# First product of a graph layer: pauses of the second and third part's ordering without work of the part behind them, and own-edge products one block behind VectorE

## The chip, the cores and the metric

The kernel runs on one core of a Trainium2 chip. The metric is the device time of one execution in microseconds (us). One execution was taken by the hardware profiler; every stretch and duration below is from it, with times counted from the start of its span. Engines are named as in the profile: PE (TensorE, matrix products), PEld (its weight loads), DVE (VectorE), ACT (ScalarE), POOL (GpSimd), SP (SyncE, which only issues transfers here).

## The reference, cut to what matters

```python
def _spmm_plus_eye(rows, cols, vals, X):          # 12500 rows of 256, 212500 edges
    msgs = vals[:, None] * X[cols]
    return jax.ops.segment_sum(msgs, rows, num_segments=N) + X
support = feature @ W1
out = _spmm_plus_eye(rows, cols, vals, support)
out = _batchnorm_relu(out, gamma, beta)
out = _spmm_plus_eye(rows, cols, vals, out @ W2)
x = x + gnn(layernorm(x), src, dst, edge_weight)
x = x + moe(layernorm(x))                          # 8 experts, the best 2 of each row
```

The edges come in no useful order for the chip: the kernel orders them itself by target row. 12500 of them are own edges (source row = target row); the rest are drawn at random.

## The kernel before

**The ordering.** The edges lie in 13 slots of 128 x 128, cut into four parts of 2, 3, 4 and 4 slots (`parts[0]` to `parts[3]`, called a, b, c, d here). Each part is ordered on the chip by a network of compare-and-exchange steps (`network`, L783). One `exchange` is, on DVE, a comparison (L641), a minimum (L643), a maximum (L645) and two predicated copies (L648, L650); ACT copies one operand of each pair aside first (L628, L632, L633). Between some steps the layout is turned by `swap` (L724): PE transposes into PSUM (L731) and ACT copies back (L734, L737). Before that come the keys (`make_keys`, L573, seven DVE instructions over the whole part). After it, ACT's counts (L598) are summed (`counted`, L601), the starts of the tiles are worked out (`begins`, L887) and the ordered list goes to DRAM slot by slot (`decode`, L848, stores at L867).

**The first product** (`spmm4`, L365) takes the lists one after the other: a, b, c, then d. It works in blocks of 128 edges: 269, 391, 513 and 513 of them. One block is a gather of 128 table rows on POOL (L215, `gt`), a selection matrix made by DVE six blocks ahead (L420, `sel`) and one to a few products on PE (L463). Every 11 to 21 blocks (four target tiles) SP loads a stretch of the list (L383), PE transposes it (L393) and DVE writes the gather's row numbers (L404, `wat`) and two more rows (L406, L408); DVE adds finished tiles (L1220). `gt` has 12 buffers, `sel` 10.

**What stands beside it.** While list a is multiplied, part b is ordered; beside b, part c; beside c, part d. The order of the instructions is written out by hand: after each block `beside()` (L1271) calls `now.give(RATE[i])`, with `RATE` 1.3, 1.15 and 1.05 us per block in the three stages. A `Beside` (L1032) keeps a ledger: what it was allowed and what it has spent, in estimated us that the generators yield (an exchange of n columns counts 0.1 + 0.00104 n for each of its first three instructions). It issues work until spent reaches allowed. A generator yields `SWAP` = 5.0 and `LEAD` = 2.5 where it has to wait for a turning; until the allowance has caught up, it issues nothing. `settle()` finishes an exchange that stands half done, and `rest()` (L1068), called after the last block of a stage, issues all that is left before the next stage begins.

**Fills.** A `Beside` with a `fill` hands the allowance on while it pauses:

```python
            if not self.gens or self.spent > self.allowed + LEAD / 2:
                if self.fill:
                    self.fill.give(us)
                return
```

L1176 makes c the fill of b and d the fill of c; L1240 makes the merging of a and b the fill of d. So c may be worked on while b pauses, and d while c pauses or is done. In the third stage (i = 2) d's generators are followed by the offsets of all lists (`beyond_all`, L1229) and by the own-edge weights of lists a, b and c (L1269).

**Own edges.** `self_weights` (L1015) loads the end of a list, where the own edges stand, and adds their weights into `selfw`, 128 rows by 98 tiles. For each block of 128 edges (18, 25, 33 and 33 for the four lists) `self_block` (L248) makes two matrices on DVE, `sel` (L251) and `tosel` (L253), and PE multiplies them into one PSUM tile (L254); both matrices come from a pool of two buffers. One addition (L1029) ends each list. List d's own edges are done beside the fourth product (L1377), at 1.0 us per block, with the rest issued when the second group of tiles begins.

Behind the third stage stand two loops over what did not fit (`self_beyond`, L266, and `beyond`, L219). They ran no turn in this execution, but all engines read their counts and branch there. The fourth product, the first projection and the merging of the lists follow, then batch norm, the second product and the experts.

Of the kernel before, what the change touches and what calls it, by code (L numbers as in the profile page):

```python
# [9 lines left out]
F32 = mybir.dt.float32  # L10
# [14 lines left out]
def kernel(  # L25
# [30 lines left out]
    nc = tc.nc  # L56
# [188 lines left out]
                    to = acc_flat[:, ds(col, F)]  # L245
                    nc.vector.tensor_tensor(to, pg, to, op=ALU.add)

    def self_block(pool, row, tile, w, ps, first, last):  # L248

        sel = pool.tile([P, P], F32, name="sel")  # L250
        nc.vector.tensor_single_scalar(sel, iota_row, row, op=ALU.is_equal)  # L251
        to = pool.tile([P, NT], F32, name="tosel")
        nc.vector.tensor_scalar(to, iota_t, tile, w, op0=ALU.is_equal, op1=ALU.mult)  # L253
        nc.tensor.matmul(ps, sel, to, start=first, stop=last)  # L254

    def self_rows(pool, win, n):

        at = pool.tile([P, 2, n], I32, name=f"sat{n}")
        rt = pool.tile([P, 2, n], F32, name=f"srt{n}")
        nc.vector.tensor_copy(at[:, 0, :], win[:, :, 1].bitcast(F32))  # L260
        nc.vector.tensor_single_scalar(at[:, 1, :], at[:, 0, :], LG, op=ALU.logical_shift_right)
        nc.vector.tensor_single_scalar(at[:, 0, :], at[:, 0, :], P - 1, op=ALU.bitwise_and)
        nc.vector.tensor_copy(rt, at)
        return rt

    def self_beyond():  # L266


        with tc.tile_pool(name="slp", bufs=1) as op, \
                tc.tile_pool(name="ps_v", bufs=1, space=PSUM) as pso:  # L270
            n = nc.values_load(most[0:1, 1:2], min_val=0, max_val=E // P + 1)
            with tc.For_i(0, n, 1):
                for lst in lists:
                    at = nc.values_load(lst.selfs[0:1, 1:2], engines=(mybir.EngineType.SP,),
                                        min_val=0, max_val=lst.FRONT + lst.size)
                    win = op.tile([P, 1, 3], I32, name="win")
                    nc.sync.dma_start(win[:, 0, :], lst.edges[ds(at, P), :])
                    rt = self_rows(op, win, 1)
                    ps = pso.tile([P, NT], F32, name="ps")
                    self_block(op, rt[:, 0, :], rt[:, 1, :], win[:, 0, 2:3].bitcast(F32), ps, True,  # L280
                               True)
                    nc.vector.tensor_tensor(selfw, selfw, ps, op=ALU.add)
                    nc.vector.tensor_scalar(lst.selfs[:, 1:2], lst.selfs[:, 1:2], P,
                                            lst.FRONT + lst.size, op0=ALU.add, op1=ALU.min)
# [496 lines left out]
    SWAP, LEAD = 5.0, 2.5  # L781

    def network(p, ring):  # L783

        for k in range(1, LG):
            for j in reversed(range(k)):
                yield from exchange(p, bit(j, k))
                yield "step"
        for j in reversed(range(LG)):
            yield from exchange(p, bit(j))  # L790
            yield "step"
        where, top = p.where, (p.n - 1).bit_length()
        for k in range(LG + 1, 2 * LG + top + 1):
            r = k - 2 * LG
            yield LEAD
            if r < 0:
                swap(p, ring, row_bits(k - LG - 1))
            elif r == 0:
                swap(p, ring, row_to_slot)
            else:  # L800
                swap(p, ring, slot_signs({where[i] for i in range(1 << top) if where[i] is not None
                                          and ((i >> (r - 1)) ^ (i >> r if r < top else 0)) & 1}))
            yield SWAP
            for j in reversed(range(r)):
                prs = slot_step(where, j, lambda i: r < top and i >> r & 1)
                yield from exchange_slots([((p, a), (p, b)) for a, b in prs])
                yield "step"
            for j in reversed(range(min(LG, k - LG))):
                yield from exchange(p, bit(j))
                yield "step"  # L810
            yield LEAD
            swap(p, ring)
            yield SWAP
            for j in reversed(range(LG)):
                yield from exchange(p, bit(j))
                yield "step"
# [198 lines left out]
    def self_weights(lst, pool, pairs, psl):  # L1015

        at = nc.values_load(lst.starts[0:1, lst.NS:], engines=(mybir.EngineType.SP,), min_val=0,
                            max_val=lst.FRONT + lst.size)
        win = pool.tile([P, lst.NSB, 3], I32, name=f"swin{lst.name}")
        nc.sync.dma_start(win, lst.edges[ds(at, lst.NSB * P), :].rearrange("(p b) r -> p b r", p=P))  # L1020
        yield SWAP
        ps = psl.tile([P, NT], F32, name="psl")
        rt = self_rows(pool, win, lst.NSB)
        yield 0.8
        for b in range(lst.NSB):
            self_block(pairs, rt[:, 0, b:b + 1], rt[:, 1, b:b + 1], win[:, b, 2:3].bitcast(F32), ps,
                       b == 0, b == lst.NSB - 1)
            yield 0.7
        nc.vector.tensor_tensor(selfw, selfw, ps, op=ALU.add)  # L1029
        yield 0.3  # L1030

# [60 lines left out]
    with ExitStack() as stack, tc.tile_pool(name="ln", bufs=1) as lp, tc.manual_schedule():  # L1092
# [80 lines left out]
        nc.vector.memset(less, 0.0)  # L1173

        work = [Beside(p.make_keys(), network(p, ringb)) for p in parts]
        work[1].fill, work[2].fill = work[2], work[3]  # L1176
        for c in parts[0].make_keys():
            pass
        clock, first, half = 0.0, 12.0, None
# [61 lines left out]
        for i in range(3):  # L1241
# [26 lines left out]
            if i == 2:  # L1268
                now.gens += [beyond_all()] + [self_weights(lst, slp, sap, psl) for lst in lists[:3]]  # L1269
# [12 lines left out]


    self_beyond()
    beyond(lists, most[0:1, 0:1], tab1)
    stats = accp.tile([P, KF, len(groups), nc.vector.BN_STATS_DIM], F32, name="stats")
    with ExitStack() as stack, tc.manual_schedule():
# [85 lines left out]

        back = Beside(merges())
        selfb = Beside(self_weights(lists[3], slp, sap, psl))

        def beside():  # L1377
# [36 lines left out]
    with tc.tile_pool(name="bn1", bufs=1) as b1p, \  # L1414
# [11 lines left out]
        for g0, n in groups:  # L1426
# [3 lines left out]
            for c0 in range(0, n, 2):  # L1430
                m = min(2, n - c0)
                ps = psb.tile([P, 2, F], F32, name="ps")
                for c in range(c0, c0 + m):
                    for k in range(KF):
                        nc.tensor.matmul(ps[:, c - c0, :], accT[:, k, g0 + c, :], wg2[:, k, :],
                                         start=(k == 0), stop=(k == KF - 1))
# [234 lines left out]
```

## Time and profile before

| | |
|---|---|
| median of 11 runs | 4880.34 us (4869.77 to 4885.23) |
| profiled execution | 4875.12 us, span 4873.4 us |
| mean granted PE clock over the span | 0.947 |
| busy over the span | PE 83%, PEld 58%, DVE 72%, ACT 31%, POOL 68% |
| gathers of the first product | 1686, mean 978 ns |
| own-edge products (L254) | 109 blocks |

How to read it: shares are over the whole span, whose second half (experts) has other limits than the stages of the first product. A time of "idle before" belongs to the engine that waited, with what ended the wait behind the arrow. A wait for several things is put down to the last of them.

### The profile page before, as it was taken

The page shows a single profiled execution, that of the slowest core. Times are in us where ns is not written, and L with a number is a line of the kernel's source. Part 1 is how long each engine was busy: PE and PEld are TensorE (multiplying, and loading weights), DVE is VectorE, ACT ScalarE, POOL GpSimd, SP SyncE. Part 2 cuts the span into 40 slices and gives each one's busy share as a digit, 9 for nine tenths or more (in the row PEclk, how much of TensorE's full clock was granted, in tenths as well). Part 3 has the DMA queues.
Part 4 walks back from the last instruction along what each step waited for, and adds up shares of the span by engine and source line. Part 5 has one row for each costly group of instructions (what it writes and reads, how often), then busy time and mean ns, then how long its engine had stood idle before and what let it go on. Part 6 is the DMA issues. An engine that isn't in the chain of part 4 may idle for free. (4 is left out here: it accounts for less than half of the span.)

```text
span 4873.4 us, 60974 instructions
## 1 busy us (share of the span) xinstructions
PE 4059.7 (83%) x15678; PEld 2843.8 (58%) x15678; DVE 3487.6 (72%) x11649; ACT 1532.5 (31%) x3783; POOL 3332.2 (68%) x3364
## 2 busy tenths in 40 slices
PE   0167768887777778888787899999999999999999
PEld 0045545554444455555465667767777777777777
DVE  9888988888787857676744566666666666666666
ACT  4767655654555001111130111211211212212223
POOL 0067757777777767777735777777777777777772
PEclk9998888989898889999998999999999999999999
DMA  4333333333333433343454343343343433433431
GB/s 134 110 90 99 98 87 106 106 111 104 106 106 105 110 100 118 118 121 117 117 175 135 113 126 115 112 126 115 113 128 114 126 116 114 127 115 115 125 106 48
DMA packets 284573, 551.61 MB, mean 113 GB/s; under 512 B 78202, under 2 KB 176612, under 8 KB 284100
## 3 DMA queue, kind: packets, MB, share of 16 engines
q0 software_dynamic: 160656, 438.91, 31.0%
q1 hardware_dynamic: 119684, 103.53, 7.0%
q10 hardware_dynamic: 3888, 5.24, 0.3%
q8 instruction: 134, 2.20, 0.2%
q14 instruction: 211, 1.73, 0.1%
HBM read 503.54 MB, written 43.91 MB: 112 GB/s over the span
## 5 line engine op out<-in xcount | busy, mean ns | idle before, releaser
L215 POOL DMA_INDIRECT gt<-tab,wat x1686 | 1648.9, 978 | 837.7 <-DMA raw<-lista 262.9
L215 POOL DMA_INDIRECT gt<-tab,win x1661 | 1680.7, 1012 | 626.7 <-issue 236.1
L463 PE MATMUL pg<-gt,sel 128*128 128x256 f32 x4826 | 1474.5, 434 | 346.9 <-DMA gt<-tab,wat 234.1
L463 PEld LDWEIGHTS pg<-gt,sel 128*128 128x128 f32 x4826 | 912.9, 210 | 791.6 <-DVE sel L420 187.8
L343 PE MATMUL pg<-gt,sel 128*128 128x256 f32 x3322 | 893.8, 387 | 92.7 <-DMA gt<-tab,win 50.5
L343 PEld LDWEIGHTS pg<-gt,sel 128*128 128x128 f32 x3322 | 620.5, 192 | 372.3 <-issue 121.4
L1581 PE MATMUL ph<-tT,w1s 128*128 128x512 f32 (+3 forms) x1728 | 742.8, 554 | 2.0 <-ACT h L1583 2.0
L1590 PE MATMUL py<-w2s,h 128*128 128x256 f32 x3136 | 744.4, 381 | 0.0
L1595 DVE SCALAR_TENSOR_TENSOR y<-py,cmb,y 128x256 f32<-128x256 f32 x784 | 343.9, 479 | 558.1 <-PE py L1590 557.6
L1583 ACT ACTIVATE h<-ph,b1s 128x512 f32<-128x512 f32 (+3 forms) x432 | 278.8, 647 | 1273.5 <-PE ph L1581 1270.0
L420 DVE TENSOR_SCALAR sel<-iota_all,wrel,wwt 128x128 f32<-128x128 f32 (+1 forms) x1686 | 630.1, 388 | 53.4 <-PE pg L463 52.3
L1590 PEld LDWEIGHTS py<-w2s,h 128*128 128x128 f32 x3136 | 600.2, 192 | 81.4
L210 DVE TENSOR_SCALAR sel<-iota_all,rel,win 128x128 f32<-128x128 f32 x1661 | 532.5, 370 | 127.4 <-PE pg L343 117.6
L1581 PEld LDWEIGHTS ph<-tT,w1s 128*128 128x128 f32 x1728 | 322.8, 191 | 203.2 <-issue 169.2
L1573 DVE SCALAR_TENSOR_TENSOR y<-b2s,cmb,y 128x256 f32<-128x256 f32 x784 | 328.3, 480 | 0.2
L731 PE MATMUL pt<-ident,keya 128*128 128x128 f32 x40 | 12.6, 416 | 218.1 <-DVE keya L645 211.1
L731 PEld LDWEIGHTS pt<-ident,keya 128*128 128x128 f32 x40 | 6.6, 207 | 223.8 <-issue 189.8
L1220 DVE TENSOR_TENSOR acc<-pg,acc 128x512 f32<-128x512 f32 x147 | 101.1, 688 | 33.4 <-PE pg L463 33.2
L1344 DVE BATCH_NORM_STATS2 stats<-po 128x6 f32<-128x512 f32 (+1 forms) x50 | 34.2, 684 | 125.8 <-ACT acc L1339 125.7
L1583 ACT ACT_TABLE_LOAD x53 | 68.0, 1283 | 174.7 <-PE ph L1581 174.6
L641 DVE TENSOR_TENSOR maskd<-keyd,opk 128x256 uint16<-128x256 f32 (+1 forms) x154 | 59.1, 383 | 56.9 <-ACT opk L628 51.0
L1336 PE MATMUL po<-aT,wg 128*128 128x512 f32 (+1 forms) x200 | 94.4, 594 | 4.7 <-DVE stats L1344 2.3
(448 smaller groups left out, 4310.3 us busy)
## 6 DMA issues: line engine op xcount, KB each, us to landing
gt<-tab,wat POOLq DMA_INDIRECT x1686, 2.8
gt<-tab,win POOLq DMA_INDIRECT x1661, 2.8
tab<-acc SPq DMA_DIRECT2D x48, 512.0 KB
own<-tab SPq DMA_DIRECT2D x46, 512.0 KB
acc<-in_x_dram SPq DMA_DIRECT2D x24, 512.0 KB
y<-in_x_dram SPq DMA_DIRECT2D x22, 512.0 KB
out_dram<-y SPq DMA_DIRECT2D x22, 512.0 KB
listm<-rec ACTq DMA_DIRECT2D x13, 192.0 KB
```

Source lines behind the costliest of these rows:

```text
L210: nc.vector.tensor_scalar(sel, iota_row, rel, w, op0=ALU.is_equal, op1=ALU.mult)
L215: nc.gpsimd.indirect_dma_start(out=gt, out_offset=None, in_=table, in_offset=bass.IndirectOffsetOnAxis(ap=at, axis=0))
L343: nc.tensor.matmul(state["ps"], sels.pop(0), gt, start=(j == 0), stop=(j == lst.blocks(t) - 1))
L420: nc.vector.tensor_scalar(sel[:, :n * P], iota_all[:, (mine[0] - g0) * P:(mine[-1] - g0 + 1) * P], rel[:, b:b + 1], w[:, b:b + 1], op0=ALU ...
L463: nc.tensor.matmul(ps[:, t - pair, :], sel[:, i * P:(i + 1) * P], gt, start=False, stop=not left)
L1220: nc.vector.tensor_tensor(acc[:, t:t + m, :], ps[:, :m, :], acc[:, t:t + m, :], op=ALU.add)
L1336: nc.tensor.matmul(po[:, :T], wg1[:, k, j * P:(j + 1) * P], aT[0][:, k, :T], start=(k == 0), stop=(k == KF - 1))
L1573: nc.vector.scalar_tensor_tensor(y[:, c, :], b2s[:, e, :], v["cmb"][:, c, e:e + 1], y[:, c, :], op0=ALU.mult, op1=ALU.add)
L1581: nc.tensor.matmul(ph[:, :T], w1s[:, e, k, j * P:(j + 1) * P], v["zT"][:, k, :T], start=(k == 0), stop=(k == KF - 1))
L1583: nc.scalar.activation(v[e][:, j, :T], ph[:, :T], AF.Gelu, bias=b1s[:, e, j:j + 1])
L1590: nc.tensor.matmul(py[:, c - c0, :], v[e][:, k, c * P:(c + 1) * P], w2s[:, e, k, :], start=(k == 0), stop=(k == KF - 1))
L1595: nc.vector.scalar_tensor_tensor(y[:, c, :], py[:, c - c0, :], v["cmb"][:, c, e:e + 1], y[:, c, :], op0=ALU.mult, op1=ALU.add)
```

## The change

L1176 goes, so that neither c nor d is any other part's fill; the merging stays the fill of d. `self_block` only makes its two matrices and hands them back. In `self_weights` the product of block b - 1 is issued after the matrices of block b, one more turn of the loop issues the last product, each turn is charged 1.0 in place of 0.7, and a `SWAP` of 5.0 is charged ahead of the addition. `self_beyond` keeps its order.

```diff
-    def self_block(pool, row, tile, w, ps, first, last):
+    def self_block(pool, row, tile, w):
...
         nc.vector.tensor_scalar(to, iota_t, tile, w, op0=ALU.is_equal, op1=ALU.mult)
-        nc.tensor.matmul(ps, sel, to, start=first, stop=last)
+        return sel, to
...
-        for b in range(lst.NSB):
-            self_block(pairs, rt[:, 0, b:b + 1], rt[:, 1, b:b + 1], win[:, b, 2:3].bitcast(F32), ps,
-                       b == 0, b == lst.NSB - 1)
-            yield 0.7
+        made = []
+        for b in range(lst.NSB + 1):
+            if b < lst.NSB:
+                made.append(self_block(pairs, rt[:, 0, b:b + 1], rt[:, 1, b:b + 1],
+                                       win[:, b, 2:3].bitcast(F32)))
+            if b:
+                nc.tensor.matmul(ps, *made.pop(0), start=(b == 1), stop=(b == lst.NSB))
+            yield 1.0
+        yield SWAP
         nc.vector.tensor_tensor(selfw, selfw, ps, op=ALU.add)
...
         work = [Beside(p.make_keys(), network(p, ringb)) for p in parts]
-        work[1].fill, work[2].fill = work[2], work[3]
```

Both programs hold the same instructions; only their order on each engine differs.

More of the change, by code (lines that the diff above doesn't have):

```diff
@@ L279, in self_beyond @@
                     ps = pso.tile([P, NT], F32, name="ps")
-                    self_block(op, rt[:, 0, :], rt[:, 1, :], win[:, 0, 2:3].bitcast(F32), ps, True,
-                               True)
+                    sel, to = self_block(op, rt[:, 0, :], rt[:, 1, :], win[:, 0, 2:3].bitcast(F32))
+                    nc.tensor.matmul(ps, sel, to, start=True, stop=True)
                     nc.vector.tensor_tensor(selfw, selfw, ps, op=ALU.add)
```

## The prediction

> **What bounds the kernel now.** The change touches the first product, so I read that stage by stage, not the shares of the span. First view: the busy time of each engine in the four products and the three gaps between them (start:end, length, then PE, PEld, DVE, ACT, POOL, PE clock).
>
> ```profile
> 265.90:623.70 357.80, 276.90 (x1039) 193.49 (x1039) 326.25 (x1195) 255.63 (x860) 258.12 (x269) 0.88 0.35 100
> 623.70:650.10 26.40, 8.61 (x24) 5.59 (x23) 18.21 (x77) 10.76 (x34) 0.02 (x1) 0.56 0.10 32
> 650.10:1142.30 492.20, 396.45 (x1458) 258.41 (x1458) 428.20 (x1439) 277.87 (x798) 373.33 (x391) 0.90 0.37 108
> 1142.30:1145.90 3.60, 2.12 (x9) 1.03 (x8) 1.04 (x5) 0.42 (x2) 0.03 (x1) 0.93 0.14 39
> 1145.90:1797.60 651.70, 513.51 (x1822) 321.88 (x1822) 506.44 (x1820) 231.50 (x641) 493.60 (x513) 0.89 0.37 106
> 1797.60:1809.90 12.30, 2.45 (x9) 1.04 (x8) 2.61 (x10) 0.00 (x0) 0.05 (x2) 0.63 0.11 29
> ```
>
> No engine is full in the second and third product, and yet they can't go faster: the timeline of POOL shows gathers of 0.95 us with 0.30 us between them, start to start 1.25 (median 1.251), and never less.
>
> ```profile
> 1794.17 0.95 POOL L215 DMA_INDIRECT gt<-tab,wat  x1 [0.30 <-issue]
> 1795.42 0.95 POOL L215 DMA_INDIRECT gt<-tab,wat  x1 [0.30 <-PE pg L463]
> 1796.67 0.95 POOL L215 DMA_INDIRECT gt<-tab,wat  x1 [0.30 <-PE pg L463]
> 1809.87 1.05 POOL L215 DMA_INDIRECT gt<-tab,wat  x1 [12.25 <-DVE sel L420]
> ```
>
> So the gathers alone need 269 x 1.251 = 336.5, 391 x 1.251 = 489.1, 513 x 1.251 = 641.8 us. Against that the products took 357.8 (21 more), 492.2 (3 more) and 651.7 (10 more). Only in the first does something else set the pace. The waits of that window say what:
>
> ```profile
> POOL gt L215 <- DVE wat L404: 14.6, 7, 4.1
> POOL gt L215 <- DVE wwt L408: 6.2, 2, 3.9
> DVE maskc L641 <- ACT opk L628: 18.7, 14, 2.7
> ```
>
> POOL waited 20.8 us in 9 places for the row numbers, behind which DVE was late, and DVE itself stood 18.7 us in c's exchanges for ACT's copies. One such place in the timeline of all engines:
>
> ```profile
> 481.40 0.29 DVE L650 COPY_PREDICATED wtsc<-maskc,opw 128x128 f32<-128x128 uint16 x1
> 481.60 0.17 DVE L404 TENSOR_SCALAR wat<-pt 128x11 int32<-128x11 int32 x1
> ...
> 482.04 0.95 POOL L215 DMA_INDIRECT gt<-tab,wat  x1 [3.95 <-DVE wwt L408]
> ```
>
> Work of part c, put into a pause of b, stands directly ahead of the row numbers. The gaps between products count in full: POOL is idle, and all that follows waits.
>
> **The change part by part.** The ledger first, as it decides where each instruction stands; it follows from the costs in the code. Before, c and d entered the second and third product, their own, with 45.4 and 100.2 us already spent; now with nothing.
> - The second product allows 391 x 1.15 = 449.7; c's keys, network, counts and list sum to 443.7. It fits: c's list ends at block 386 of 391 (before at 349).
> - The third allows 513 x 1.05 = 538.7. Before, 590.0 - 100.2 = 489.8 fell due in it, done at block 468. Now d's 100.2 come back, the own edges of a, b, c are charged 76 x 0.3 + 3 x (1.0 + 5.0) = 40.8 more, and 16.8 fall away, since 21 more counts go with the blocks and not as 0.8 each: 614. About 75 don't fit: 23 of b's 25 own-edge blocks and all 33 of c's (29.3 and 45.1 with what stands around them), 56 blocks. `rest()` issues them after the last gather.
>
> *First product, -18.3.* 154 DVE instructions of c and d go: 14 exchange steps of ten (2.0 us each, as from 625.4 to 627.4) and two sets of keys (3.8 us each, the first from 312.7), 36 us together, and with them the 18.7 us of waits. DVE falls from 326 to some 290 of 336. I leave 3 of the 21 us, what the second product loses at about the same DVE share: 339.5 instead of 357.8. Bounds: -21 and, if b's own dense stretches fill DVE, 0.
>
> *Gap 623.7 to 650.1, -4.* One exchange of c stands in it (625.4 to 627.4, 2 us) and DVE enters it late: the turning of b that belongs to block 263 ran at 622.6, as the last gather did. Bounds -7 and 0.
>
> *Second product, 0* (-3 to +3): gathers bound it, DVE loses work.
>
> *Gap 1142.3 to 1145.9, +1.* The chain from b's count (the memset L604 at 639.59) to the next gather (650.08) takes 10.5 us; c's fourth slot adds a store, some 2 us. It now starts at block 381, ten gathers (12.5 us) before the end, plus 2.9 us from a gather's start to its product. It comes out level with the 3.6 us that the last products cost anyway. Bounds 0 and +10.5.
>
> *Third product, -1.5.* DVE gets some 24 us more (272 instructions of d, 65 us, against the pairs of 62 own-edge blocks, 30, and merging, 11): about 530 of 642. Its dense stretches stay as they were. The 10 us of loss lie mostly around 1600 to 1700, offsets and a's own edges, where POOL waited 2.4 us once for the products L254; those are now charged 1.0. Bounds -10 and +5.
>
> *Gap 1797.6 to 1809.9, +43.* Now DVE is idle here: its last addition starts at 1800.29, list d is loaded at 1805.70, row numbers at 1807.95. With the change DVE's queue holds 56 blocks of own edges between that addition and the loops, and every engine branches in those loops before d's first load. No gather hides it. The nearest row is the run of such blocks at 1838.8 to 1845.8, where only they are issued. First DVE's timeline, starts of `sel`:
>
> ```profile
> 1842.20 0.29 DVE L251 TENSOR_SCALAR sel<-iota_all,srt 128x128 f32<-128x128 f32 x1
> ...
> 1843.07 0.43 DVE L251 TENSOR_SCALAR sel<-iota_all,srt 128x128 f32<-128x128 f32 x1 [0.32 <-PE psl L254]
> ...
> 1843.59 0.29 DVE L251 TENSOR_SCALAR sel<-iota_all,srt 128x128 f32<-128x128 f32 x1
> ...
> 1844.44 0.32 DVE L251 TENSOR_SCALAR sel<-iota_all,srt 128x128 f32<-128x128 f32 x1 [0.32 <-PE psl L254]
> ```
>
> Then the window, with PE and PEld first and the granted clock, 0.50, third from the end:
>
> ```profile
> 1842.20:1845.80 3.60, 3.31 (x11) 2.60 (x11) 2.13 (x9) 0.00 (x0) 2.69 (x4) 0.50 0.34 97
> ```
>
> Its fastest blocks take 0.44, DVE's own pace; the last three average 0.75, at clock 0.50, where DVE waits for the product that frees the two buffers. PE's last eight products took 5.34 us, 0.67 each; I take that: 56 x 0.67 = 37.5. The new order changes nothing here, as nothing stands between the products on PE. Added: c's row numbers 0.9, two additions that wait for the last product 2 x 1.1. Sum 40.6. Behind the loops four exchanges of the merging (a and b, twice) remain, 5.1 us by b's 1.54 and a's 1.0, against 2.25 us that DVE waits there now: +2.9. Together 43; bounds 56 x 0.44 and 56 x 0.75, so +30 to +48. Below that a gain is excluded: the queue is in order.
>
> [...] The row shows the array at half clock within such a run, though PE was busy for 3.31 of 3.60 us. [...]
>
> *Fourth product, +1* (-3 to +5). By block 21 six fewer of d's 33 own-edge blocks are made, so the burst at 1838.8 grows from 11 to 17 blocks, 4 us; gathers run up to 12 blocks ahead and did not wait there before. PE's waits for `tosel` shrink (11.0 us in 7 places, no gather behind most).
>
> Sum: -18.3 - 4 + 0 + 1 - 1.5 + 43 + 1 = **+21 us**. On the profiled execution's 4875.1 (span 4873.4) that is 4896; it ran 5.2 us under the median of 4880.3, so I forecast 4901 for the median.
>
> **The rivals.**
> - *VectorE's pace sets the tail.* 56 x 0.44 = 24.6 instead of 37.5: +8, 4888, no change. For: DVE was the slower engine at clock 0.93. Against: the clock fell within 4 us.
> - *The first stage keeps its waits* (b alone saturates DVE, which was 95% busy from 266 to 320, nearly without c): no -18 and no -4, +43, 4923. Against: each wait followed work of c or d.
> - *List c comes late*, if its count slips behind the last gather: 10 us more, 4911, and 4924 if the whole 26.4 us gap of list b repeats.
> - *Faster: VectorE gets to the tail before the gathers end.* It is idle for 145 of 652 us in the third product; if it ran over 31 us ahead (past -0.2%), and with all 43 hidden, the sum is -22, 4858. Against: block 2 of the tail needs the buffer that the product of block 0 frees, which PE reaches behind the last gather's landing.
>
> **How the numbers follow.** Chances: forecast 0.62, VectorE's pace 0.13, waits kept 0.12, list c late 0.08, tail hidden 0.05. A measurement of this kernel tells about 0.2% (10 us) from no change: faster 0.05, same 0.15 (the second case and the low edge of the first), slower 0.80. The range runs from +2, under the case at VectorE's pace, to +42, just below waits kept: 4882 to 4922. The forecast's own range is 4890 to 4911.
>
> **What would show it.** First product near 340, no POOL wait on L404 there; second 492; gap behind it under 6; third near 650; the gap before list d near 55, with 56 own-edge blocks in it. I am wrong if the clock stays open in that gap (then 40 to 46), or if the gap isn't there at all.

## The result and the profile after

The changed kernel takes 4896.71 us (median of 8 runs, 4892.48 to 4903.23) against 4880.30 before (31 runs): a ratio of 1.0037, 95% interval 1.0029 to 1.0046. It is slower by 16.4 us; 4901 was forecast. The profiled execution has a span of 4890.6 us, 17.2 more than before (4873.4).

The same view as before the change: busy time by stretch (start:end, length, then PE, PEld, DVE, ACT, POOL, granted PE clock). The first six lines answer to the six of the kernel before, the seventh is the fourth product.

```profile
265.70:603.70 338.00, 283.01 (x1052) 186.99 (x1052) 294.65 (x1050) 236.39 (x782) 256.34 (x269) 0.90 0.37 106
603.70:624.90 21.20, 3.67 (x14) 1.90 (x12) 13.08 (x57) 6.66 (x20) 0.00 (x0) 0.64 0.12 38
624.90:1118.00 493.10, 403.24 (x1430) 259.63 (x1430) 406.28 (x1331) 251.79 (x718) 374.28 (x391) 0.87 0.37 107
1118.00:1122.00 4.00, 2.91 (x12) 1.41 (x10) 1.04 (x5) 0.00 (x0) 0.04 (x2) 0.96 0.24 66
1122.00:1769.50 647.50, 514.49 (x1732) 317.01 (x1732) 533.60 (x1954) 276.61 (x805) 491.50 (x513) 0.86 0.38 107
1769.50:1827.00 57.50, 37.60 (x125) 28.79 (x124) 36.21 (x148) 2.83 (x9) 0.00 (x0) 0.51 0.06 16
1827.00:2508.80 681.80, 568.87 (x2057) 366.02 (x2058) 478.34 (x1537) 104.35 (x239) 523.57 (x513) 0.92 0.41 121
```

The view shows a gain and a loss of nearly twice its size. The first product fell from 357.8 to 338.0 and the gap behind it from 26.4 to 21.2: 25 us gained. The gap before list d grew from 12.2 to 57.5: 45.3 lost. The other stretches moved by 4.3 us at most.

The gain: these are POOL's waits in the first product (us in total, times, longest). The 20.8 us behind the row numbers (L404, L408) are gone; what is left is 0.30 between two gathers.

```profile
POOL gt L215 <- issue: 41.1, 135, 0.3
POOL gt L215 <- PE pg L463: 32.3, 106, 0.3
```

The loss: POOL's timeline around the gap, the last gather of the third product and the first of the fourth.

```profile
1768.55 0.95 POOL L215 DMA_INDIRECT gt<-tab,wat  x1 [0.30 <-PE pg L463]
1827.02 0.97 POOL L215 DMA_INDIRECT gt<-tab,wat  x1 [57.53 <-DVE sel L420]
```

Between them DVE makes exactly 56 own-edge blocks, called the tail below. The first one's `sel` starts at 1773.25, the last one's at 1812.57. Four of them in its timeline (L1031 is the product that was L254):

```profile
1776.42 0.28 DVE L251 TENSOR_SCALAR sel<-iota_all,srt 128x128 f32<-128x128 f32 x1
...
1777.35 0.29 DVE L251 TENSOR_SCALAR sel<-iota_all,srt 128x128 f32<-128x128 f32 x1 [0.40 <-PE psl L1031]
...
1777.79 0.28 DVE L251 TENSOR_SCALAR sel<-iota_all,srt 128x128 f32<-128x128 f32 x1
...
1778.71 0.29 DVE L251 TENSOR_SCALAR sel<-iota_all,srt 128x128 f32<-128x128 f32 x1 [0.40 <-PE psl L1031]
```

Two blocks take 1.37 us, 0.684 each, and every second one waits 0.40 us for a product. The clock stays at half all that time (PE first, clock third from the end):

```profile
1776.00:1784.00 8.00, 6.91 (x25) 5.43 (x24) 5.79 (x24) 0.00 (x0) 0.00 (x0) 0.50 0.00 0
```

### The profile page after: what moved, and what is told of

It reads as the page before. It is cut to its first block, busy times and chain, and to the rows that moved or that the text cites. A ratio compares the mean times of both kernels' runs of the same rounds, so it can differ in the third digit from the quotient of the medians.

```text
span 4890.6 us, 61067 instructions
## 1 busy us (share of the span) xinstructions
PE 4116.8 (84%) x15678; PEld 2868.9 (59%) x15678; DVE 3491.8 (71%) x11649; ACT 1530.8 (31%) x3783; POOL 3326.1 (68%) x3364
## 5 line engine op out<-in xcount | busy, mean ns | idle before, releaser
L463 PE MATMUL pg<-gt,sel 128*128 128x256 f32 x4826 | 1511.9, 442 | 360.4 <-DMA gt<-tab,wat 257.9
L343 PE MATMUL pg<-gt,sel 128*128 128x256 f32 x3322 | 894.8, 388 | 87.7 <-DMA gt<-tab,win 44.7
L420 DVE TENSOR_SCALAR sel<-iota_all,wrel,wwt 128x128 f32<-128x128 f32 (+1 forms) x1686 | 630.6, 389 | 55.8 <-PE pg L463 54.8
L731 PE MATMUL pt<-ident,keya 128*128 128x128 f32 x40 | 12.4, 408 | 218.0 <-DVE keya L645 211.0
L628 ACT COPY opk<-keyb 128x192 f32<-128x192 f32 (+1 forms) x148 | 46.0, 311 | 176.5 <-DVE keya L645 152.0
```

What stands on the lines that cost most here:

```text
L343: nc.tensor.matmul(state["ps"], sels.pop(0), gt, start=(j == 0), stop=(j == lst.blocks(t) - 1))
L420: nc.vector.tensor_scalar(sel[:, :n * P], iota_all[:, (mine[0] - g0) * P:(mine[-1] - g0 + 1) * P], rel[:, b:b + 1], w[:, b:b + 1], op0=ALU ...
L463: nc.tensor.matmul(ps[:, t - pair, :], sel[:, i * P:(i + 1) * P], gt, start=False, stop=not left)
```

## The experiments

Theory: the fill links' end makes the gain (VectorE is no longer late with row numbers), and on the ledger it makes the loss (work that c and d had done early now falls due in the third product, and 56 blocks don't fit). Rivals: the products one block behind, or their dearer charge, make the loss; or VectorE has no room for the blocks anyway.

The runs went to several chips. The first two groups met chips on which the kernel before takes 5502 and 5550 us (the last section says what their profiles show); the third and fourth group met 4875 and 4874 us, like the first measurements. A ratio compares with the kernel before on the same chip. The changed kernel itself was not run on the slower chips. The stretches below are from one profiled execution each and worked as above: the three products, each followed by its gap.

| run | ratio (95%) | first, gap | second, gap | third, gap |
|---|---|---|---|---|
| before | 1 | 357.8, 26.4 | 492.2, 3.6 | 651.8, 12.2 |
| changed | 1.0037 (1.0029 to 1.0046) | 338.0, 21.2 | 493.1, 4.0 | 647.5, 57.5 |
| chips of 4874 to 4875 us: | | | | |
| e2c_lag_only | 1.0000 (0.9991 to 1.0009) | 357.5, 26.4 | 491.6, 3.6 | 652.1, 12.3 |
| e4c_rate | 0.9960 (0.9946 to 0.9974) | 338.1, 21.0 | 492.9, 3.8 | 656.4, 12.2 |
| e7_fills_rate | 0.9964 (0.9950 to 0.9977) | 339.5, 21.2 | 494.2, 3.8 | 661.6, 12.2 |
| e10_best | 0.9928 (0.9914 to 0.9941) | 339.0, 7.8 | 494.2, 7.5 | 647.3, 12.2 |
| chip of 5502 us: | | | | |
| e1_fills_only | 1.0043 (1.0027 to 1.0060) | 410.4, 25.2 | 579.8, 8.7 | 795.0, 55.8 |
| e2_lag_only | 1.0022 (1.0010 to 1.0034) | 433.7, 26.4 | 589.8, 8.3 | 794.5, 12.4 |
| e4_rate | 1.0021 (1.0008 to 1.0033) | 409.8, 25.4 | 574.3, 9.9 | 820.8, 12.1 |
| e5_bufs | 1.0045 (1.0029 to 1.0061) | 408.6, 24.0 | 586.9, 8.0 | 792.1, 48.1 |
| chip of 5550 us: | | | | |
| e2b_lag_only | 1.0020 (1.0006 to 1.0034) | 430.9, 26.4 | 592.3, 9.0 | 799.2, 12.3 |
| e3_c_fill_off | 0.9978 (0.9967 to 0.9988) | 421.0, 24.7 | 617.2, 10.1 | 792.8, 12.9 |
| e4b_rate | 1.0031 (1.0017 to 1.0045) | 418.3, 24.8 | 593.7, 12.9 | 833.7, 12.7 |
| e9_rates | 1.0021 (1.0009 to 1.0033) | 427.8, 6.5 | 601.0, 4.5 | 825.5, 12.2 |

**One part alone: the products a block behind** (e2, e2b, e2c). The changed kernel with the links back in:

```diff
+        work[1].fill, work[2].fill = work[2], work[3]
```

> The other part alone: the changed kernel with the two fill links back in. All own edges then fit (the list of what is due ends at block 507 of 513). Theory: first product 358 and its gap 26 as before, no run of blocks before list d (gap near 12); only the third product may lose what the products a block behind save, 0 to 4 us; time 4876 to 4880. Rival (the products a block behind, or their dearer charge, make the loss in the gap): gap near 57, time near 4925. Rival (the dearer charge crowds the third product): third product 655 to 660, time 4884 to 4889.

> The products one block behind alone (fill links kept), once more for the same reason. Theory: first product 358, gap 26, gap before list d 12, third product 648 to 652, time 4876 to 4880, no change. Rival (dearer charge or the delay costs something): third product 655 to 660 or gap near 57, time 4884 to 4925.

> The products one block behind alone, fill links kept, for a chip that runs the kernel before in 4875 to 4880 us. Theory: first product 358, gap 26, gap before list d 12, third product 647 to 652 (the version made to beat both has 647.3 without this part, so its gain is small): 0 to 4 us less than before, no change. Rival (the dearer charge crowds the third product's end: done at block 507 instead of 468): third product 655 to 660, 4 to 9 us more than before. Rival (this part makes the gap of 57.5): time 45 us above before.

Measured on a chip like that of the first measurements: 1.0000, and each stretch of the table within 0.6 us of before. This part alone does nothing there, neither gain nor loss, and the dearer charge fits the ledger while the links are in. It doesn't even cure the one wait that it might be meant for. POOL's waits for the own-edge products in the third product were 10.0 us in 26 places before, the longest 2.4 us; here they are

```profile
POOL gt L215 <- PE psl L1031: 13.2, 34, 3.2
```

The products stand in PE's queue among those of the gathered blocks as before, only one block later; that this is why the wait stays is not shown. On the two slower chips it cost 0.2% by the ratios (14 and 7 us by the medians); where, the stretches don't say, as no profile of the kernel before was taken there.

**The other part alone: the links out** (e1), from the kernel before:

```diff
-        work[1].fill, work[2].fill = work[2], work[3]
```

> One part alone: the two fill links are taken out of the kernel before, and its own-edge blocks stay as they were (product right behind its block, 0.7 on the ledger). By the costs in the code 39 own-edge blocks (6 of b, 33 of c) don't fit in the third product, against 56 in the changed kernel. Theory (the links give the gain of the first product, and the blocks that no longer fit give the loss): first product near 338, gap behind it near 21, 39 x 0.684 us (the changed kernel's tail) = 26.7 in the gap before list d, which is then near 46 where the changed kernel has 57.5; time near 4897 - 11.6 = 4885, up to 4 more if the 4.3 us gained in the third product come from the products a block behind. Rival (the products a block behind make the loss): the gap is near 12 as before, time near 4855. Rival (each block is cheaper when its product follows at once, 0.44): gap near 37, time near 4876.

The ratio, 1.0043, can't be told apart from the changed kernel's 1.0037; some 1.001 was expected. Against e2 on the same chip the first product is 23 us shorter and the gap before list d 43 us longer. Those two runs differ by both parts of the change. But on good chips e2c and the changed kernel differ by the links alone, and there the first product goes from 357.5 to 338.0 and the gap before list d from 12.3 to 57.5. So without the links both the gain and the loss appear. The loss is not the links' alone in full, however: on the ledger the dearer charge adds 17 of the 56 blocks, some 12 us at 0.684 each, once the links are out. No run on a good chip has the links out with the old charge and the old allowance, so this share is not measured. Here the gap of 55.8 was to be 46: this chip's VectorE was behind when the gathers ended and made 52 blocks after them, not 39 (e5, with the dearer charge, made 58 on this chip). Its last 33, with each product right behind its block, took 0.684 us each again; the order of the products doesn't touch the pace.

**The shortfall taken away** (e4, e4b, e4c), from the changed kernel:

```diff
-        RATE = (1.3, 1.15, 1.05)
+        RATE = (1.3, 1.15, 1.25)
```

> The changed kernel with the allowance of the third product raised from 1.05 to 1.25 us per block (641 us in all, where 625 fall due; done at block 501 of 513). Nothing else differs. Theory (the loss is 56 blocks that the allowance shut out, although VectorE has the time): no run of own-edge blocks in the gap, which falls from 57.5 to near 12; third product 647 to 652; time 4897 - 45 = 4852 (4848 to 4858), below both kernels. Rival (VectorE has no room for them beside the gathers): the gap goes, but the third product grows by what went, to 670 or more, time 4875 to 4897.

> The changed kernel with 1.25 instead of 1.05 us of allowance per block of the third product once more, since the chip of the first group ran the kernel before in 5502 us (engines stood still for 1 to 5 us at a time, releaser issue or unknown) and there the third product took 821 against 795 us with the tail. Theory, if engines don't stop like that: 45 us less than the changed kernel, 28 us (0.6%) less than before: third product 647 to 655, gap behind it near 12, time 4852. Rival (VectorE has no room for the 56 blocks beside the gathers, as the 821 us would say): third product longer by 26 or more, near 675, gap near 12, time near 4878, as before.

> The changed kernel with 1.25 instead of 1.05 us of allowance per block of the third product, for a chip that runs the kernel before in 4875 to 4880 us, as the third group's did. It stands beside the run with the same rate, no fill links and the own edges as before (4858, third product 661.6, gap before list d 12.2), so the two differ by the products a block behind, charged 1.0 each. Theory: gap before list d 12, third product 648 to 655, since the own-edge products no longer stand ahead of gathered blocks in one place for 3.7 us; time 4848 to 4855, 41 to 49 us below the changed kernel. Rival (VectorE has no room at the higher rate): third product 660 to 675, time 4860 to 4878. If the shortfall on the ledger were not the cause of the gap of 57.5, the gap would stay.

In all three the gap is back at 12 to 13. The third product and its gap in e4c_rate, as in the first view:

```profile
1121.10:1777.60 656.50, 518.79 (x1848) 332.06 (x1848) 567.85 (x2092) 281.38 (x814) 492.79 (x513) 0.88 0.37 106
1777.60:1789.80 12.20, 2.41 (x9) 1.04 (x8) 2.58 (x10) 0.00 (x0) 0.00 (x0) 0.65 0.15 33
```

So the allowance shut the blocks out, and nothing else. On the good chip the gain is kept (4856.15 us, 0.9960), yet the third product took 656.4 and not 648 to 655; on the slow chips it took 26 to 35 us more than with the links in. The theory holds for the gap, and the rival is right in part. On the good chip most of what the third product lost is in one place. POOL's timeline of e4c_rate:

```profile
1652.63 0.96 POOL L215 DMA_INDIRECT gt<-tab,wat  x1 [0.30 <-PE pg L463]
1660.43 0.94 POOL L215 DMA_INDIRECT gt<-tab,wat  x1 [6.83 <-issue]
```

and VectorE's timeline ahead of it, where the row numbers (L404) stand behind the offsets of list d:

```profile
1651.09 0.42 DVE L989 SCALAR_TENSOR_TENSOR ojunk<-oend,oixd,ones_t 128x196 f32<-128x196 f32 x1
...
1656.82 0.42 DVE L992 SCALAR_TENSOR_TENSOR ojunk<-oend,oixd,step__141 128x196 f32<-128x196 f32 x1
...
1659.51 0.18 DVE L404 TENSOR_SCALAR wat<-pt 128x21 int32<-128x21 int32 x1
```

The next gather was due at 1653.9; DVE had no idle time from 1651 on, and came to `wat` at 1659.5. The label "issue" only says that no other releaser was found; the timeline of DVE shows the cause. It is the mechanism of the first product's lost 20 us again: work that the raised allowance puts ahead of the row numbers makes VectorE late with them.

**The same rate without the products a block behind** (e7): the kernel before, links out, third allowance 1.25.

> The kernel before without its fill links, own edges as before (0.7 each), and 1.25 instead of 1.05 us of allowance per block of the third product. 584 of 641 us fall due, done at block 468. No tail by the ledger. On a chip that runs the kernel before in 4880 us: theory (the blocks were only shut out by the allowance) first product 338, gap 21, third 648 to 655, gap 12, time 4852 to 4858; rival (VectorE has no room for the added work at the higher rate) third 675 or more, time 4878 or more. On a chip like those of the first two groups (5500 to 5550, the higher rate cost 26 to 34 us in the third product with the products a block behind): if the rate is what costs, third 820 to 835 here too; if the products a block behind cost it, third near 795.

The time, 4858.3 us, is at the upper end of the theory. The third product, 661.6, lies between theory and rival, with the same wait of 6.84 us behind list d's offsets and one of 3.7 behind own-edge products, which e4c_rate doesn't have (its longest is 0.3). The ratios of the two runs, 0.9964 and 0.9960, can't be told apart.

**The tail's pace** (e5): the changed kernel, with a pool of four buffers for the pair of matrices.

```diff
+            tc.tile_pool(name="selfs4", bufs=4) as sap4, tc.manual_schedule():
...
-                now.gens += [beyond_all()] + [self_weights(lst, slp, sap, psl) for lst in lists[:3]]
+                now.gens += [beyond_all()] + [self_weights(lst, slp, sap4, psl) for lst in lists[:3]]
```

> The changed kernel with four buffers instead of two for the pair of 0/1 matrices of an own-edge block (beside products one to three). The 56 blocks still run in the gap. Theory (in that run VectorE waits for the product that frees a buffer, and TensorE at half clock sets the pace): the waits of VectorE for the buffers go to the ends of the run, TensorE is busy throughout, and a block takes what it takes on TensorE, 6.91 us busy in 8 us x 0.684 = 0.59 instead of 0.684: gap near 52, time near 4891. If TensorE, busy all the time, is granted the full clock, VectorE's 0.44 sets the pace: gap near 44, time near 4883. Rival (VectorE's own work is the pace): no change, gap 57, time 4897.

Of the two readings in the theory, the first missed (0.59 a block), and the second was right on the pace of 0.44 but not on its condition, the full clock. VectorE's waits in the tail, first of the changed kernel, then of e5_bufs:

```profile
DVE sel L251 <- PE psl L1031: 10.8, 27, 0.4
```

```profile
DVE selfw L1034 <- PE psl L1031: 1.4, 2, 0.8
```

The waits of `sel` for buffers are gone (what is left is the wait of two additions, which the changed kernel has too), and blocks come every 0.44 us (`sel` in VectorE's timeline of e5_bufs):

```profile
2094.36 0.28 DVE L251 TENSOR_SCALAR sel<-iota_all,srt 128x128 f32<-128x128 f32 x1
...
2094.79 0.28 DVE L251 TENSOR_SCALAR sel<-iota_all,srt 128x128 f32<-128x128 f32 x1
...
2095.23 0.28 DVE L251 TENSOR_SCALAR sel<-iota_all,srt 128x128 f32<-128x128 f32 x1
```

And they do so while the clock is still at half, as the windows of e5_bufs show (PE first, DVE third, clock third from the end):

```profile
2092.00:2098.00 6.00, 6.00 (x29) 6.00 (x29) 6.00 (x29) 0.00 (x0) 0.00 (x0) 0.50 0.00 0
2108.00:2114.00 6.00, 6.00 (x29) 4.05 (x29) 6.00 (x29) 0.00 (x0) 0.00 (x0) 1.00 0.01 3
```

VectorE is busy for 6.00 of 6.00 us and the pace is the same at both clocks, so the pace is VectorE's own, and TensorE at half clock does keep up with it. (PE's 6.00 of 6.00 at both clocks says that its records overlap, not that it is at its limit.) The 0.684 was no throughput: with two buffers it is the round trip from a finished pair over its product back to a free buffer. At a higher clock the trip was shorter. In e1_fills_only, with two buffers too and no gather beside them, two blocks took 1.09 us at a clock of 0.98 (`sel` at 2098.01 and 2099.10; the clock is that of 2094 to 2102) and 1.37 at 0.50 (2104.40 and 2105.77; 2102 to 2110). In the kernel before, also with two buffers but with gathers beside them, six blocks from 1838.76 to 1842.20 took 0.57 us each at a clock of 0.93:

```profile
1838.76 0.28 DVE L251 TENSOR_SCALAR sel<-iota_all,srt 128x128 f32<-128x128 f32 x1 [0.31 <-PE psl L254]
...
1842.20 0.29 DVE L251 TENSOR_SCALAR sel<-iota_all,srt 128x128 f32<-128x128 f32 x1
```

```profile
1838.70:1842.20 3.50, 2.71 (x13) 1.66 (x11) 3.28 (x12) 0.00 (x0) 2.87 (x3) 0.93 0.39 112
```

The gap of e5_bufs was 48.1, and would have been near 45 with the changed kernel's 5.3 us in the loops (8.5 here). What the buffers are worth in the whole time is not shown, as the changed kernel was not run on this chip.

**Only c out of b's pauses** (e3), from the kernel before:

```diff
-        work[1].fill, work[2].fill = work[2], work[3]
+        work[2].fill = work[3]
```

> The kernel before with only the first of the two fill links gone: b's pauses take nothing of c, c's pauses still take d's work, own edges as before. d then enters the third product with 56.6 us spent and all fits (582 of 595 due, done at block 501): no tail. Theory (the first product's gain comes from c's work gone from b's pauses; the loss only from what doesn't fit): first product near 338, gap near 21, second 492 to 496, gap 4, third 650 to 655, gap 12; 25 us less than before, 4855. Rival (d's work in c's pauses, now beside all of c, makes list c late): gap behind the second product 10 to 26, time 4861 to 4880.

No tail (12.9), and faster than before, 0.9978; 12 us by the interval's middle where 25 were expected. Against e2b on the same chip, the first product and its gap are 12 us shorter and the second product 25 longer; the profiled execution of e3 is 18 us above its own median, so that the second product's loss is not settled here. The version at the end, e10, has the same link out on a good chip, and its second product is only 2 us longer than before.

**More allowance for b and c** (e9), from the changed kernel:

```diff
-        RATE = (1.3, 1.15, 1.05)
+        RATE = (1.4, 1.2, 1.25)
```

> The changed kernel with allowances of 1.4, 1.2 and 1.25 us per block instead of 1.3, 1.15 and 1.05. b's work, 394.6 us by the costs in the code against 376.7 allowed, then ends at block 263 of 269 in place of behind the last gather. Theory (the gap behind the first product is list b's shortfall on the same ledger, and VectorE, 295 of 338 us busy, has the room): gap 21 falls to 4 to 8, first product 338 to 342, second 490 to 494, third 647 to 655, no tail; 4840 (4834 to 4850). Rival (VectorE is full in the first product at the higher rate): what leaves the gap comes back as waits for row numbers, first product 350 to 355; time near 4852, that of the run with the third allowance alone.

The gap behind the first product fell to 6.5, so it was b's own shortfall on the ledger. Against e4b on the same chip, first and second product gave back 10 and 7 of the 18 and 8 us that the two gaps lost, and the intervals of the two ratios overlap.

**A version that beats both** (e10): e3 with the first two of these allowances.

```diff
-        work[1].fill, work[2].fill = work[2], work[3]
+        work[2].fill = work[3]
...
-        RATE = (1.3, 1.15, 1.05)
+        RATE = (1.4, 1.2, 1.05)
```

> A version made to beat both kernels: the kernel before, only the first fill link gone, and allowances of 1.4, 1.2 and 1.05 us per block instead of 1.3, 1.15 and 1.05. By the costs in the code b's list ends at block 263 of 269, c's at 370 of 391, d enters the third product with 76 us spent, and all is done there at block 487 of 513; no tail. On a chip that runs the kernel before in 4880 us: theory first product 338 to 342, gap 4 to 8 instead of 26, second 492 to 496, gap 4, third 650 to 655, gap 12; 35 to 42 us less than before, 4838 to 4845. Rival (VectorE is full in the first product at the higher rate): first product back at 350 to 358, time 4855 to 4860. On a chip with the pauses of the first two groups: 20 to 40 us less than before.

4838.85 us against 4875.18, 0.9928: 36 us below before, in the forecast 35 to 42. Busy time by stretch, as in the first view:

```profile
265.60:604.60 339.00, 276.49 (x1055) 192.70 (x1055) 305.35 (x1099) 241.70 (x800) 256.97 (x269) 0.90 0.37 106
604.60:612.50 7.90, 2.82 (x11) 1.16 (x9) 2.09 (x8) 0.37 (x1) 0.08 (x1) 0.89 0.33 106
...
1114.20:1761.50 647.30, 510.19 (x1844) 322.21 (x1844) 510.86 (x1840) 239.14 (x663) 491.33 (x513) 0.89 0.38 107
1761.50:1773.70 12.20, 2.44 (x9) 1.04 (x8) 2.56 (x10) 0.00 (x0) 0.00 (x0) 0.76 0.18 28
```

The first product holds more of b's work (DVE 305 against 295 in the changed kernel) and is only 1 us longer for it. d's early start is kept, only taken from c's pauses, where VectorE had slack (busy for 452.2 of 494.2 us of e10's second product), and all 76 own-edge blocks lie under the third product. The gap behind the second product, 7.5, is longer than the 4 that was expected.

## Why the prediction held, point by point

The time was right (4897 for 4901), and so was the sum: +17 us profiled for +21. The misses of the single terms, 3 us at most, partly cancel. By its terms:

- *First product, -18.3*: -19.8. The reason held: no wait for row numbers is left, and e2c, with the links, has its 357.5 back. But VectorE's waits for ScalarE's copies (`maskc`, 18.7 us) did not go: in b's exchanges they grew from 4.5 to 28.5 us. They cost nothing, as VectorE is no longer late with the row numbers. The 3 us of leave for b's own dense stretches were mostly not needed; the gathers run at 1.251 us start to start, with 1.8 us of loss in 269.
- *Gap behind it, -4*: -5.2. That what remains is b's own work was not said; e9 and e10, where a larger allowance brings it to 6.5 and 7.8, show it.
- *Second product, 0, and gap, +1*: +0.9 and +0.4.
- *Third product, -1.5*: -4.3, mis-sized, and the reason given (a's own edges "are now charged 1.0") fell. e2c has that charge and takes 652.1; e10 has neither charge nor delay and takes 647.3 with all blocks. Of the 4.3 us, 2.1 are before's one long wait behind own-edge products at 1680 (2.4 in place of 0.30), which the changed kernel and e10 both lack. What the rest is stays open.
- *Gap before list d, +43*: +45.3, the term that decides the sign. The ledger gave 23 + 33 blocks, and 56 stand in the trace; e4c removes them by the allowance alone, and the 45.3 with them. At 0.684 us the blocks took 38.3 where 37.5 was worked out. The step that failed is the mechanism behind the price: the last eight products of the row were taken as what TensorE needs at half clock. e5 shows that it keeps up with 0.44 at half clock. The 0.24 on top come with the two buffers, and there was more of it at half clock (0.684 a block) than at 0.93 (0.57) or 0.98 (0.545 in e1_fills_only). So the clock mattered for the price, but not because TensorE was the slower engine. That 0.67 came so near to 0.684 is luck in part: it averages eight products from 1840.43 on, of which the first three started before the clock fell (0.88 from 1840.3 to 1842.2). The case "VectorE's pace sets the tail" was argued over the clock alone; e5 brings it about at half clock, with two more buffers.
- *The clock in that gap*: the row of the kernel before had it at half, and half it was, 0.50 over the 40 us of the tail. For a clock that stays open 40 to 46 us of gap were given; no run shows this tail, with its two buffers, at full clock, and the nearest measured are the 0.545 us a block of e1_fills_only at 0.98, which make 30.5 us for 56 blocks.
- *Fourth product, +1*: +2.1, of no more than single executions' weight. The burst of list d's own edges did grow to 17 blocks. That gathers don't wait there did not hold: behind it two gathers waited 1.26 and 1.56 us in place of 0.30. *The rest of the program* wasn't in the sum: -2.0, inside the 5.6 us by which that unchanged stretch differs between the six profiled executions on good chips (2381.8 to 2387.4).

Of the rivals, the waits kept in the first stage, list c late and the hidden tail did not happen. The forecast's question, whether VectorE's 145 idle us in the third product can take the tail, has the answer of e4c: the 56 blocks fit, for 8.9 us of a longer third product.

## What to carry to other kernels

Work that is done early in another stage's pauses is a loan on that stage's allowance: take it back out, and count what then falls due behind the last transfer, where it costs its whole length (56 blocks made the gap 45.3 us longer here). Raise an allowance only after looking at what stands ahead of the instruction that the bound engine waits for (here the row numbers), and let early work go where the engine that does it has slack. When a run of small blocks is slower than the engine that makes them, try more buffers (here four in place of two, 0.44 us a block for 0.684) before blaming the other engine.

## What the runs showed of the hardware

- The clock: in the changed kernel's tail PE was busy for 33.1 of 40.1 us by its records (1773.25 to 1813.35; 6.91 of 8 in the window above), and the clock stayed at 0.50. In e5, with PE's records without a break for 10.3 us from 2088.8, it stayed at 0.50 too; after a pause of 1.7 us and a fresh start at 2100.84 it opened at about 2107.6, 6.8 us later (the window from 2107.0 to 2107.5 shows 0.50, the next half microsecond 0.89). What made it open there and not before, the runs don't show.
- Chips differ. On two of them the same program took 12.9 and 13.9% longer than the 4874 to 4875 us seen elsewhere. The gathers' usual step was 1.25 us there too (e1_fills_only, 322.77 to 419.47), and VectorE was busy as long (405.9 us in its second product of 579.8, 406.3 in the changed kernel's of 493.1), so the engines wait longer. In some places several of them stood still together, in e1_fills_only PE, its weight loads, VectorE and POOL from 350.63 to 351.29 for instance. Part of POOL's waits, 30.0 us in the second product, is put down to "remote", a releaser that the profile doesn't name. The granted clock over the span was lower too (0.881 against 0.947); whether that is cause or consequence is open. POOL's waits of e1_fills_only in the second product, where in the changed kernel no gather waits more than 0.31 us:

```profile
POOL gt L215 <- PE pg L463: 59.8, 57, 8.9
POOL gt L215 <- remote: 30.0, 23, 3.5
```

There the third product at the raised allowance took 26 and 35 us more than with the links in, against 4 on a good chip, and the products a block behind cost 0.2% instead of nothing. Why these chips wait was not found. The raised allowance (e4) is a gain of 0.4% on a good chip and a loss of 0.2 to 0.3% on these, so such a plan is to be measured on more than one chip.
